# Query, key and value by 26 block products with shared token sums on GpSimd, and every order written anew

## The chip, the core and the metric

The kernel runs on one core of one Trainium2 chip. A core has five engines that run side by side, each through its own queue in the order of the program: TensorE (PE: matrix products into the eight banks of PSUM; its weight loads are shown as PEld), VectorE (DVE), ScalarE (ACT), GpSimd (POOL), and SyncE (SP), whose queue issues nearly all DMA transfers here. The engines wait for one another by semaphores. The metric is the device time of one execution in microseconds.

## The reference

128 graphs of 128 nodes with 512 features go through two layers; all is float32.

```python
# layer 0
h = jnp.maximum(_layernorm(x, axis=-1), 0.0)
q, k, v = (proj(Wq, bq), proj(Wk, bk), proj(Wv, bv))          # 8 heads of 64
scores = jnp.einsum('bhqd,bhkd->bhqk', q, k) * SCALE
scores = scores * (adj + adj)[:, None, :, :]
attn = jax.nn.softmax(scores, axis=-1)
x = x + (jnp.einsum('bhqk,bhkd->bhqd', attn, v) as rows) @ Wo.T + bo
# layer 1
h = jnp.maximum(_layernorm(x, axis=-1), 0.0)
Wh = h @ W;  e = leaky_relu(Wh @ a[:512] + (Wh @ a[512:]).T, 0.2)
attention = softmax(where(adj > 0.5, e, -9e15), axis=1)
x = x + elu(attention @ Wh)
```

(The lines of the softmaxes and of the last sum are shortened here.)

## The kernel before

Graphs are handled in pairs `p` (64 of them) and, for query, key and value, in groups `g` of two pairs (32 of them). A group's normalised and transposed input is the tile `hA`: features on the partitions, four feature blocks of 128, and 256 token columns for each of the two pairs.

The products with `wq`, `wk`, `wv` and, for each pair, with `wo` and `w1` are done by a fast 2x2 scheme. Every matrix is cut into two by two quarters, and seven products of sums of quarters stand for eight plain ones (`PRODUCTS`, L130). The sums of weight quarters are formed once on VectorE (`weight_sum`, L137). The sums of token quarters are formed for each group (`token_sum` called by `hidden_sum`, tile `hS`), and for each pair on the context `cxT` and on the gathered input `gT` (steps `cs`, `gs`). A product of a group is the function `product` (L239 on): four matmuls over 256 columns at L258, accumulated in three banks a, b and c for each of query, key and value. Bank a holds running sums: it is read after four of the seven products, by ScalarE (the function `first`, L270 and L275, with the bias), while banks b and c are added to the result in SBUF by VectorE (`add`, L279), three times for each of query, key and value.

Before these products a pair's input is normalised in its transposed form (`hidden`): step `hd0` subtracts the row means (L222, VectorE, 1024 elements), step `hd1` takes the maximum with zero and multiplies (L224). The rows' statistics come from steps `t0` and `t1` (L165, L166), a small power on GpSimd (L172, L173), and a trip through DRAM (`s0` on GpSimd's queue, `f0` on SP's). Step `sh` adds the vector `c` to a pair's `x` after it was loaded by step `lx` (L234, VectorE).

Attention of a graph (`a` and `b` in step names are the two graphs of a pair): scores (`sc`, L320, two banks), times adjacency (`at`, L327, VectorE), maxima (`mx`, L334), exponentials (`ex`, L339, ScalarE), shares and normalising (`rc` L343, `nm` L348), block transposition on VectorE (`fl`, L355) and through DRAM (`bl`, `pl` on SP's queue), context (`pc`, L388) and its copy by ScalarE into `cxT` (`pe`, L395). Output of layer 0: products `o0` to `o6` (L299), added to `x` by VectorE (`od`, L402). Layer 1: statistics `st`, hidden values `h2` (L418), dot products with the attention vectors (`d`, L425, VectorE), mask, softmax (`wm` L455, `pr` L460, `m1` L464, `e1` L469, `sw` L474 and L475), gathering (`g`, L481, TensorE) and its copy (`ge`, L487), products `w0` to `w6` (L299), collected by ScalarE (`zc`, L495) and VectorE (`wd`, L499), then `ez` (L507), `fa` (L511), `fb` (L515) and the store `so`.

The order of the work on all queues is written out by hand as three lists of steps: `HEAD` once, `ORDER` for each pair `p` from 3 to 59 (the number after the colon is how many pairs behind the step works), and `TAIL` once. Steps `U1` to `U11` are the 21 products of the next group, ten in an even round and eleven in an odd one; `F` and `A` are their takes by ScalarE and VectorE. All PSUM tiles come from one pool of eight banks, `ps1`. TensorE's product waits until the bank it writes is free[...].

Of the kernel before, what the change touches and what calls it, by code (L numbers as in the profile page):

```python
# [8 lines left out]
F32 = mybir.dt.float32  # L9
# [4 lines left out]
P = 128  # L14
# [10 lines left out]
def kernel(  # L25
# [6 lines left out]
    wqT: bass.AP,  # L32
    bq: bass.AP,
    wkT: bass.AP,
    bk: bass.AP,
    wvT: bass.AP,
# [23 lines left out]
    xs, x0s, adjs, adjTs, hAs, hSs = {}, {}, {}, {}, {}, {}  # L60
# [18 lines left out]
    def half_of_hidden(p):  # L79

        g, i = divmod(p, 2)
        if g not in hAs:
            hAs[g] = grp.tile([P, 4, 2, 2 * S], F32, name="hA")
        return hAs[g][:, 2 * i : 2 * i + 2].rearrange("p q c k -> p (q c) k")
# [19 lines left out]
    def column(src, name):  # L104
# [10 lines left out]
    wv_sb, wq_sb, wk_sb, wo_sb, w1_sb = (  # L115
        const.tile([P, 7, 2, E // 2], F32, name=name) for name in ("wv", "wq", "wk", "wo", "w1")
    )
# [16 lines left out]
    FIRSTS = {0: (0, 0), 2: (1, 0), 4: (1, 1), 5: (0, 1)}  # L134
    ADDS = {1: (0, 0, "b"), 4: (1, 1, "c"), 6: (1, 0, "c")}
# [12 lines left out]
    def token_sum(h, s, k):  # L148

        if k == 0:  # L150
            nc.vector.tensor_tensor(s[:, 0], h[:, 2], h[:, 3], OP.add)
        elif k == 1:
            nc.vector.tensor_tensor(s[:, 1], s[:, 0], h[:, 0], OP.subtract)  # L153
        elif k == 2:
            nc.vector.tensor_tensor(s[:, 2], h[:, 0], h[:, 2], OP.subtract)
        else:
            nc.vector.tensor_tensor(h[:, 2], h[:, 1], s[:, 1], OP.subtract)
# [59 lines left out]
    def hidden(p, k):  # L217

        h = hAs[p // 2][:, 2 * (p % 2) : 2 * (p % 2) + 2].rearrange("p q c k -> p (q c) k")
        row = rows0[p][:, None, :, k].to_broadcast([P, 2 * 2, 2 * S])  # L220
        if k == 0:
            nc.vector.tensor_tensor(h, h, row, OP.subtract)  # L222
        else:
            nc.vector.scalar_tensor_tensor(h, h, 0.0, row, op0=OP.max, op1=OP.mult)  # L224

    def hidden_sum(g, k):
        if g not in hSs:
            hSs[g] = grp.tile([P, 3, 2, 2 * S], F32, name="hS")
        token_sum(hAs[g], hSs[g], k)

    def shift(p):


        nc.vector.tensor_tensor(xs[p], xs[p], c_sb[:, None, :].to_broadcast([P, 2, E]), OP.add)  # L234

    accs = {}

    def product(g, which, n):

        if n == 0:  # L240
            if which == "v":
                vs[g] = grp.tile([P, G, E], F32, name="v")
            else:
                qks[g, which] = {}
        if which != "v" and n in (0, 2):
            qks[g, which][n // 2] = grp.tile([P, C, 2 * S], F32, name=which + "T", bufs=3 if which == "q" else 2)
        w = {"q": wq_sb, "k": wk_sb, "v": wv_sb}[which]
        ha, wb, bank = PRODUCTS[n]
        fresh = (g, which, bank) not in accs
        if fresh:  # L250
            accs[g, which, bank] = ps1.tile([P, 2, 2 * S], F32, name="acc_" + bank, tag="ps1")
        acc = accs[g, which, bank]
        h = hAs[g][:, ha] if ha < 4 else hSs[g][:, ha - 4]
        for m in range(2):
            ms = slice(m * P, (m + 1) * P)
            for c in range(2):
                lhsT, rhs = (h[:, c, ms], w[:, wb, c, :]) if which == "v" else (w[:, wb, c, ms], h[:, c, :])
                nc.tensor.matmul(  # L258
                    acc[:, m, :], lhsT, rhs, start=fresh and m == 0 and c == 0, stop=c == 1, skip_group_check=True
                )  # L260

        def dst(t, f):
            if which == "v":
                return vs[g][:, 2 * t : 2 * t + 2, f * 2 * P : (f + 1) * 2 * P]
            return qks[g, which][t][:, 2 * f : 2 * f + 2, :]

        def first(t, f):
            a = accs[g, which, "a"]
            if which == "v":
                nc.scalar.copy(dst(t, f), a)  # L270
            else:
                bias = bk_sb if which == "k" else bq_sb
                for m in range(2):
                    j = 2 * f + m
                    nc.scalar.activation(dst(t, f)[:, m, :], a[:, m, :], AF.Identity, bias=bias[:, j : j + 1])  # L275

        def add(t, f, bank):
            d = dst(t, f)
            nc.vector.tensor_tensor(d, accs[g, which, bank], d, OP.add)  # L279

        def firsts():
            if n in FIRSTS:
                first(*FIRSTS[n])

        def adds():
            if n in ADDS:
                add(*ADDS[n])

        return firsts, adds
# [20 lines left out]
    def scores(b):  # L310
        p, i = divmod(b, 2)
        g, h = divmod(p, 2)
        qT, kT = qks[g, "q"][h], qks[g, "k"][h]
# [80 lines left out]
    def keep_context(b):  # L394
        nc.scalar.copy(rows_of(cxT, b % 2), pcs.pop(b))  # L395
# [88 lines left out]
    def keep_gathered(p, i):  # L484
        if p not in gTs:
            gTs[p] = work.tile([P, 7, 2, S], F32, name="gT")
        nc.scalar.copy(rows_of(gTs[p], i), pgs.pop((p, i)))  # L487
# [77 lines left out]
    SEQ = "v0 v1 v2 v3 v4 q0 v5 q1 v6 q2 q3 q4 k0 q5 k1 q6 k2 k3 k4 k5 k6".split()  # L565
# [6 lines left out]
    EARLY, LATE = 3, 4  # L572

    def listed(text, mark):
# [3 lines left out]
        lx@0 lx@1 Lq1@0 Lq0@0 lx@2 Lk0@0 Lk1@0 Lv0@0 t1@-5 Lo0@0 t0@-5 pp@0 hn0@0 hn1@0 tp0@0 t0@-4 tp1@0 ev0@0 ev1@0  # L578
        t1@-4 U6@-2 Wq0@0 pp@1 Wq1@0 t1@-3 U8@-2 hn0@1 l0@-2 Wq2@0 Lv1@0 hn1@1 tp0@1 Lo1@0 U3@-1 Lw1@0 t0@-3 ev0@1 Lu@0
        Wq3@0 pp@2 tp1@1 hn1@2 U5@-1 ev1@1 hn0@2 F6@-2 Wk0@0 hs0@-3 F3@-1 U1@-2 Wk1@0 hs1@-3 hs2@-3 U10@-2 tp0@2 F10@-2  # L580
        U7@-1 t1@-2 t0@-2 U2@-1 Wv0@0 F7@-1 pp@3 Wk3@0 F1@-2 A8@-2 ev0@2 U9@-1 hn0@3 Wv1@0 hn1@3 hs3@-3 tp0@3 l0@-1
        tp1@2 Wv2@0 la@-1 U3@-2 ev1@2 Lw0@0 ev0@3 lt@0 F9@-1 tp1@3 F2@-1 ccp@0 F3@-2 ev1@3 U1@0 ccd@0 t0@-1 t1@-1 U4@-2
        Wo0@0 l0@0 s0@-1 cu10@0 U5@-2 Wv3@0 A5@-1 U4@-1 hs0@-1 U10@-1 U1@-1 F10@-1 F4@-1 ccs@0 A2@-1 cch@0 sca@0 Wk2@0
        scb@0 ata0@0 ata1@0 U6@-1 mxa@0 hs1@-1 exa2@0 U3@1 t1@0 F5@-2 exa3@0 A6@-1 U6@0 A5@-2 F1@0 Wo1@0 rca1@0 t0@0
        U9@-2 F6@0 l0@1 s0@0 exa1@0 f0@0 exa0@0 U3@0 A9@-2 nma3@0 Wo2@0 nma2@0 rca0@0 cu01@0 U10@0 nma1@0 nma0@0 hs2@-1
        F3@1 U8@0 fla@0 Ww0@0 bla@0 U8@-1 atb0@0 la@0 atb1@0 mxb@0 U5@1 A8@0 exb2@0 A9@-1 pla@0 U2@-2 exb0@0 A5@1 exb1@0
        sh@0 F10@0 U11@-1 exb3@0 rcb1@0 U7@-2 nmb3@0 A11@-1 rcb0@0 t0@1 t1@1 U2@1 F7@-2 nmb1@0 cu11@0 l0@2 s0@1 nmb2@0
        f0@1 U7@1 F3@0 lT@0 cu00@0 nmb0@0 lT@1 sca@1 A2@-2 flb@0 scb@1 pca@0 F7@1 ata0@1 blb@0 ata1@1 F2@1 U5@0 mxa@1
# [91 lines left out]
    def steps(p):  # L680
# [75 lines left out]
        if odd and (g + 2) * 2 < N:  # L756
            for k in range(4):
                table[f"hs{k}"] = lambda k=k: hidden_sum(g + 2, k)
# [70 lines left out]
```

## Time and profile before

| | |
|---|---|
| runs (3) | median 2351.17 us, 2348.68 to 2352.63 |
| profiled execution, span from first to last instruction | 2346.1 us |
| profiled execution, time of its own beside the span | the page gives none |
| TensorE busy | 2332.0 us, 99% |
| VectorE busy | 2000.4 us, 85% |
| ScalarE busy | 1467.2 us, 63% |
| GpSimd busy | 257.0 us, 11% |
| DMA | 314 MB, 134 GB/s over the span |

A line of the timeline gives start and duration in us, engine, line of the kernel, operation, the tile written and the tiles read, shapes, and how many instructions were merged (x8); in brackets stands the idle time before it and what ended it. A float32 matmul appears as two records. The ends of matmuls are modelled, so that a busy TensorE is not TensorE at its peak: the distance from one start to the next tells what a matmul costs.

### The profile page before, as it was taken

To read this page: it belongs to the slowest core of one execution; us is meant where nothing else is said; L and a number is where in the kernel's file an instruction comes from. 1 tells how busy PE (TensorE), PEld (TensorE's weight loads), DVE (VectorE), ACT (ScalarE), POOL (GpSimd) and SP (SyncE) were. 2 spreads that over 40 slices of the span, in tenths; PEclk is the share of its full clock that TensorE was granted. 3 is DMA by queue.
4 is the path that set the end of the run, shared out by engine and by line. 5 is a ranking of instruction groups with operands and counts; after the bars stand their busy time and mean duration, and the time that the engine had idled before them with its cause. 6 is when DMAs were issued, how large, how long until landed. Compare 5 with 4: busy or idle time off the path is not lost.

```text
span 2346.1 us, 41028 instructions
## 1 busy us (share of the span) xinstructions
PE 2332.0 (99%) x14184; PEld 2061.2 (88%) x14184; DVE 2000.4 (85%) x4113; ACT 1467.2 (63%) x4815; POOL 257.0 (11%) x320
## 2 busy tenths in 40 slices
PE   9999999999999999999999999999999999999998
PEld 8888888888888888888888888888888888888886
DVE  6888888888888888888888888888888888888888
ACT  3656666666566665666666666656666566666774
POOL 1101101111101011011110111110101101110000
PEclk9999999999999999999999999999999999999999
DMA  5445454454444554544535445444454453453332
GB/s 171 131 113 157 121 147 120 124 164 125 143 131 119 148 139 130 143 114 142 155 122 149 120 123 165 124 144 131 120 148 137 131 145 108 146 153 116 118 120 95
DMA packets 267351, 314.06 MB, mean 134 GB/s; under 512 B 24200, under 2 KB 192136, under 8 KB 267144
## 3 DMA queue, kind: packets, MB, share of 16 engines
q1 hardware_dynamic: 263112, 311.31, 45.0%
q8 instruction: 112, 1.84, 0.3%
q0 software_dynamic: 1920, 0.13, 0.2%
q14 instruction: 95, 0.78, 0.1%
q10 hardware_dynamic: 2112, 0.01, 0.1%
HBM read 210.51 MB, written 100.85 MB: 133 GB/s over the span
## 4 chain that ended last, share of the span: by engine, by line
PE 99%; DVE 0%; ACT 0%; DMA 0%; issue 0%; POOL 0%; SPq 0%; ACTq 0%; DVEq 0%; POOLq 0%
PE acc_a L258 29%; PE row_a L299 24%; PE acc_c L258 14%; PE row_c L299 9%; PE acc_b L258 7%; PE sc L320 5%; PE pc L388 5%; PE pg L481 5%; PE pt L197 0%; DMA x<-in_x 0%; PE pm L531 0%; DVE st L165 0%; ACT z L495 0%; PE pu L553 0%; DVE z L499 0%
## 5 line engine op out<-in xcount | busy, mean ns | idle before, releaser
L339 ACT ACTIVATE at<-at,nmx 128x128 f32<-128x128 f32 x1024 | 396.3, 390 | 19.8 <-DVE nmx L334 17.9
L348 ACT ACTIVATE at<-at,rs 128x128 f32<-128x128 f32 x1024 | 325.0, 391 | 12.8 <-DVE rs L343 12.1
L299 PE MATMUL row_a<-wo,cxT 128*128 128x256 f32 x1280 | 328.5, 379 | 0.3 <-DVE cxT L153 0.3
L299 PE MATMUL row_a<-w,gT 128*128 128x256 f32 x1280 | 319.4, 380 | 2.9 <-DVE z L499 1.7
L172 POOL TENSOR_SCALAR mv<-mv 128x2 f32<-128x2 f32 x124 | 79.2, 639 | 2016.8 <-DVE mv L166 1994.6
L299 PEld LDWEIGHTS row_a<-w,gT 128*128 128x128 f32 x1280 | 242.3, 190 | 37.9 <-DVE z L499 2.6
L299 PEld LDWEIGHTS row_a<-wo,cxT 128*128 128x128 f32 x1280 | 242.6, 190 | 34.3 <-DVE cxT L153 0.6
L402 DVE TENSOR_TENSOR x<-row_a,x 128x256 f32<-128x256 f32 x320 | 135.3, 423 | 133.1 <-PE row_a L299 129.8
L495 ACT COPY z<-row_a 128x256 f32<-128x256 f32 x256 | 94.3, 368 | 203.7 <-PE row_a L299 203.6
L275 ACT ACTIVATE kT<-acc_a,bk 128x256 f32<-128x256 f32 x256 | 106.5, 466 | 168.2 <-PE acc_a L258 165.0
L327 DVE SCALAR_TENSOR_TENSOR at<-sc,adj 128x512 f32<-128x512 f32 x256 | 165.1, 686 | 42.2 <-PE sc L320 39.8
L339 ACT ACTIVATION_READ_ACCUMULATOR at<-at,nmx 128x1 f32 x1024 | 193.3, 189 | 0.0
L275 ACT ACTIVATE qT<-acc_a,bq 128x256 f32<-128x256 f32 x256 | 106.1, 466 | 123.0 <-PE acc_a L258 123.0
L165 DVE BATCH_NORM_STATS2 st<-x 128x6 f32<-128x512 f32 x256 | 176.1, 688 | 7.4 <-DMA x<-in_x 5.1
L425 DVE SCALAR_TENSOR_TENSOR junk<-h,u 128x512 f32<-128x512 f32 x256 | 173.3, 677 | 0.6
L355 DVE STREAM_TRANSPOSE tr<-at 128x1024 f32<-128x1024 f32 x128 | 158.8, 1240 | 9.2 <-PE pc L388 2.7
L334 DVE TENSOR_REDUCE nmx<-at 128x8 f32<-128x1024 f32 x128 | 156.2, 1220 | 4.3
L487 ACT COPY gT<-pg 128x512 f32<-128x512 f32 x128 | 74.6, 584 | 123.8 <-PE pg L481 117.4
L481 PEld LDWEIGHTS pg<-w,h 128*128 128x128 f32 x1024 | 133.3, 192 | 6.6 <-ACT z L495 0.2
L173 POOL TENSOR_TENSOR mv<-mv,mhalf 128x2 f32<-128x2 f32 x128 | 131.1, 1024 | 30.7 <-DVE mv L168 20.3
L481 PE MATMUL pg<-w,h 128*128 128x128 f32 x1024 | 134.1, 275 | 0.0
L299 PE MATMUL row_c<-w,gT 128*128 128x256 f32 x512 | 133.0, 382 | 0.6 <-DVE z L499 0.5
(130 smaller groups left out, 4876.4 us busy)
## 6 DMA issues: line engine op xcount, KB each, us to landing
blocks<-tr SPq DMA_DIRECT2D x128, 512.0 KB, 6.8
aT<-blocks SPq DMA_DIRECT2D x512, 128.0 KB, 2.9
x<-in_x SPq DMA_DIRECT2D x123, 512.0 KB, 5.0
out<-x SPq DMA_DIRECT2D x63, 512.0 KB, 4.1
hA<-in_xT SPq DMA_DIRECT2D x120, 256.0 KB, 3.7
mr<-rows SPq DMA_DIRECT2D x60, 256.0 KB, 4.4
adj<-in_adj SPq DMA_DIRECT2D x64, 128.0 KB, 4.3
adjT<-in_adjT SPq DMA_DIRECT2D x64, 128.0 KB, 4.2
```

The source lines that it names most:

```text
L165: nc.vector.bn_stats(st, src[:, i, :])
L258: nc.tensor.matmul(acc[:, m, :], lhsT, rhs, start=fresh and m == 0 and c == 0, stop=c == 1, skip_group_check=True)
L275: nc.scalar.activation(dst(t, f)[:, m, :], a[:, m, :], AF.Identity, bias=bias[:, j : j + 1])
L299: nc.tensor.matmul(acc, left[:, la, c, :], w[:, wb, c, :], start=n in (0, 3) and c == 0, stop=c == 1, skip_group_check=True)
L327: nc.vector.scalar_tensor_tensor(ats[b][0][:, k * C : (k + 1) * C, :], scs[b][k], QSCALE, adjs[p][:, i : i + 1, :].to_broadcast([P, C, S]) ...
L334: nc.vector.tensor_reduce(nmx, at, AX.X, OP.max, negate=True)
L339: nc.scalar.activation(at[:, j, :], at[:, j, :], AF.Exp, bias=nmx[:, j : j + 1], accum_out=sums[:, j : j + 1])
L348: nc.scalar.activation(at[:, j, :], at[:, j, :], AF.Copy, scale=rs[:, j : j + 1])
L355: nc.vector.transpose(trs[b], at.rearrange("p h (j k) -> p j h k", k=Q))
L402: nc.vector.tensor_tensor(d, row_acc(p, "o", bank), d, OP.add)
L425: nc.vector.scalar_tensor_tensor(junk, h2[:, i, :], 1.0, u_sb[:, k, :], op0=OP.mult, op1=OP.mult, accum_out=ws[:, i, 1:2] if k else src_sb ...
L481: nc.tensor.matmul(pg[:, c, :], h1s[p][0][:, i, c * P : (c + 1) * P], wts[p][:, i, :], start=True, stop=True)
```

## The change

Query, key and value of a group are computed together by another scheme. The tokens are cut into two halves (the two pairs), the features into four blocks of 128, and the outputs into four blocks of 128. 26 products of one token sum with one weight sum stand for 32 plain ones. `TERMS` lists them in order: the accumulating chain (0 to 3), the number of the token sum, the slot of the weight sum, and where the chain's running value is taken to (token half, output block, sign; a dot takes nothing). `FORMS` lists the 17 token sums; they serve query, key and value alike and are formed by GpSimd, 256 elements each, in eight buffers. `WSUMS` lists the 35 weight sums, formed once by VectorE on the three weights together (384 elements).

Query and key share a bank, value has one of its own. Step `Q` is a product for query and key (two matmuls over 256 columns), step `V` one for value (two matmuls with the token sum as weights over 128 columns). `A` and `B` take the running value: the first time that a part of the result is written ScalarE does it, after that VectorE adds or subtracts.

The row subtraction `hd0` and the addition of `c` (`sh`) go to GpSimd, each in pieces of 512 elements. The token sums of the context and of the gathered input read three of their operands from the PSUM banks rather than from the copy in SBUF. The three lists are new; `ORDER` now covers a whole group, and runs for groups 2 to 28.

```diff
-    wv_sb, wq_sb, wk_sb, wo_sb, w1_sb = (
-        const.tile([P, 7, 2, E // 2], F32, name=name) for name in ("wv", "wq", "wk", "wo", "w1")
-    )
+    wo_sb, w1_sb = (const.tile([P, 7, 2, E // 2], F32, name=name) for name in ("wo", "w1"))
+    w_sb = const.tile([P, SLOTS, 3, P], F32, name="w3")
...
+    TERMS = list(terms("""
+        1,8,7,13- 0,10,18,10- 1,9,19,03- 0,11,0,00- 1,1,20,01+ 0,2,16,. 1,13,5,11+ 0,0,21,03- 1,12,6,12- 0,0,1,02-
+        1,14,14,02- 0,18,24,00+ 0,3,26,01+ 3,20,15,03+ 2,21,22,02- 3,19,25,13+ 2,22,23,12- 3,16,9,11- 2,6,10,.
+        3,17,27,01- 2,4,2,13+ 3,15,4,00- 2,4,3,10- 3,23,12,10- 2,24,8,12+ 2,7,13,11-
+    """))
+    FORMS = list(sums("""
+        4+5 1-8 2+9 0+9 5+7 12-1 3-13 1+2 6+12 16-15 17-3 0-18 16+19 6+19 4-19 7-17 5-1
+    """))
...
+    def load_blocks(n):
+
+        nc.sync.dma_start(w_sb[:, n : C * C : C], wT[:, n : C * C : C])
+
+    def block_sum(k):
+
+        d, a, op, b = WSUMS[k]
+        if op == "n":
+            nc.vector.scalar_tensor_tensor(w_sb[:, d], w_sb[:, a], -1.0, w_sb[:, b], op0=OP.mult, op1=OP.subtract)
+        else:
+            eng = nc.gpsimd if k in () else nc.vector
+            eng.tensor_tensor(w_sb[:, d], w_sb[:, a], w_sb[:, b], OP.add if op == "+" else OP.subtract)
...
-    def token_sum(h, s, k):
+    def token_sum(h, bank, k):
+
+        s = h[:, 4:7]
+
+        def block(q):
+            return bank(q // 2)[:, q % 2 * 2 : q % 2 * 2 + 2, :]
 
         if k == 0:
-            nc.vector.tensor_tensor(s[:, 0], h[:, 2], h[:, 3], OP.add)
+            nc.vector.tensor_tensor(s[:, 0], block(2), h[:, 3], OP.add)
         elif k == 1:
-            nc.vector.tensor_tensor(s[:, 1], s[:, 0], h[:, 0], OP.subtract)
+            nc.vector.tensor_tensor(s[:, 1], s[:, 0], block(0), OP.subtract)
         elif k == 2:
-            nc.vector.tensor_tensor(s[:, 2], h[:, 0], h[:, 2], OP.subtract)
+            nc.vector.tensor_tensor(s[:, 2], block(0), h[:, 2], OP.subtract)
         else:
-            nc.vector.tensor_tensor(h[:, 2], h[:, 1], s[:, 1], OP.subtract)
+            nc.vector.tensor_tensor(h[:, 2], block(1), s[:, 1], OP.subtract)
...
         if k == 0:
-            nc.vector.tensor_tensor(h, h, row, OP.subtract)
+            for c in range(0, C, 2):
+                nc.gpsimd.tensor_tensor(h[:, c : c + 2], h[:, c : c + 2], row[:, c : c + 2], OP.subtract)
...
-        nc.vector.tensor_tensor(xs[p], xs[p], c_sb[:, None, :].to_broadcast([P, 2, E]), OP.add)
+        for i in range(2):
+            nc.gpsimd.tensor_tensor(xs[p][:, i, :], xs[p][:, i, :], c_sb, OP.add)
...
+    def make_form(g, k):
+
+        a, op, b = FORMS[k]
+        forms[g, 2 * C + k] = grp.tile([P, 2 * S], F32, name="tf", bufs=8)
+        eng = nc.gpsimd
+        eng.tensor_tensor(forms[g, 2 * C + k], form(g, a), form(g, b), OP.add if op == "+" else OP.subtract)
...
+    def product_qk(g, n):
+
+        _, f, slot, _ = TERMS[n]
+        acc, fresh = fresh_acc(g, n, "q", [P, 2, 2 * S])
+        for i in range(2):
+            nc.tensor.matmul(
+                acc[:, i, :], w_sb[:, slot, i, :], form(g, f), start=fresh and i == 0, stop=True, skip_group_check=True
+            )
+
+    def product_v(g, n):
+
+        _, f, slot, _ = TERMS[n]
+        acc, fresh = fresh_acc(g, n, "v", [P, 2, P])
+        for i in range(2):
+            nc.tensor.matmul(
+                acc[:, i, :], form(g, f)[:, i * P : (i + 1) * P], w_sb[:, slot, 2, :],
+                start=fresh and i == 0, stop=True, skip_group_check=True,
+            )
+
+    def take_qk(g, n):
+
+        chain, _, _, (t, j, sign) = TERMS[n]
+        acc = accs[g, chain, "q"]
+        if (g, t) not in qks:
+            qks[g, t] = grp.tile([P, 2, C, 2 * S], F32, name="qk", tag=f"qk{t}", bufs=1 + t)
+        d = qks[g, t][:, :, j, :]
+        if (g, t, j) not in begun:
+            begun.add((g, t, j))
+            for i, bias in enumerate((bq_sb, bk_sb)):
+                nc.scalar.activation(d[:, i, :], acc[:, i, :], AF.Identity, bias=bias[:, j : j + 1], scale=float(sign))
+        else:
+            nc.vector.tensor_tensor(d, d, acc, OP.add if sign > 0 else OP.subtract)
+
+    def take_v(g, n):
...
+        if (g, t, j, "v") not in begun:
+            begun.add((g, t, j, "v"))
+            nc.scalar.activation(d, acc, AF.Copy, scale=float(sign))
+        else:
+            nc.vector.tensor_tensor(d, d, acc, OP.add if sign > 0 else OP.subtract)
...
-        nc.scalar.copy(rows_of(cxT, b % 2), pcs.pop(b))
+        nc.scalar.copy(rows_of(cxT, b % 2), pcs[b])
...
-    EARLY, LATE = 3, 4
+    EARLY, LATE = 2, 3
...
     ORDER = """
+        rca1:0 rca0:0 gs1:3 lx:1 sh:1 Q2:0 w0:3 Q25:2 nma2:0 V23:2 B23:2 T7:0 V25:2 A23:2 gs2:3 lt:2 lT:0 f0:0 Q1:0
+        A1:0 B25:2 pca:1 nma3:0 gs3:3 zc0:3 d10:2 d00:2 pcb:1 T5:0 peb:1 nma0:0 pea:1 d11:2 cs0:1 px:2 pd:2 scb:0
...
+        h20:1 d01:1 Q9:0 gs0:2 A9:0 Q10:0 lx:0 T12:0 V13:0 w0:2 Q13:0 zc0:2 B13:0 V15:0 V11:0 B8:0 V10:0 A10:0 t1:-2
+        gs2:2 s0:-1 gs1:2 B11:0 Q11:0 hd0:-1 hd1:-1 w2:2 l0:-3 A11:0 A13:0 h21:1 plb:0 w1:2 V12:0 Q15:0 B10:0 Q12:0
+        wd1:2 s0:-2 f0:-3 exa1:-1 exa0:-1 rca0:-1 exa2:-1 B12:0 exa3:-1 rca1:-1 nma3:-1 d00:1 d10:1 T13:0 Q14:0 A14:0
...
+        exb2:-1 exb3:-1 sh:0 rcb1:-1 cs2:0 exb0:-1 Q19:0 exb1:-1 nmb3:-1 w3:2 T14:0 V16:0 A19:0 od0:0 Q16:0 T0:-2
...
-        for p in range(EARLY, N - LATE):
+        for g in range(EARLY, N // 2 - LATE):
             for step, lag in ORDER:
-                if p >= lag:
-                    do(step, p - lag)
+                do(step, 2 * g - lag)
```

## The prediction

> **What bounds the kernel now.** I read the engines' busy times (part 1) and the chain that ended last (part 4) first, then the windows view over single rounds of the written order, the waits inside one round, and the timeline.
>
> ```profile
> PE 2332.0 (99%) x14184; PEld 2061.2 (88%) x14184; DVE 2000.4 (85%) x4113; ACT 1467.2 (63%) x4815; POOL 257.0 (11%) x320
> PE 99%; DVE 0%; ACT 0%; DMA 0%; issue 0%; POOL 0%; SPq 0%; ACTq 0%; DVEq 0%; POOLq 0%
> ```
>
> The chain is TensorE from end to end. The order repeats every group of four graphs (two pairs); one such round in the windows view (us, then busy us and instructions of PE, PEld, DVE, ACT, POOL):
>
> ```profile
> 1217.39:1289.61 72.22, 72.22 (x442) 64.03 (x441) 62.04 (x128) 45.70 (x151) 8.33 (x11) 1.00 0.47 136
> ```
>
> In that round TensorE waits for nobody; VectorE waits 8.8 us in all, most of it here (waiter, releaser: us, times, longest):
>
> ```profile
> DVE x L402 <- PE row_a L299: 4.3, 4, 2.0
> DVE x L234 <- DMA x<-in_x: 1.9, 1, 1.9
> DVE at L327 <- PE sc L320: 1.3, 2, 0.9
> ```
>
> So VectorE is occupied 72.22 - 8.8 = 63.4 us of 72.2 (88%). Since matmul ends are modelled, I price TensorE by the distance of starts, from its timeline (a float32 matmul is two records):
>
> ```profile
> 1201.84 1.89 PE L258 MATMUL acc_a<-wv,hA 128*128 128x256 f32 x8
> 1203.57 1.89 PE L258 MATMUL acc_b<-hA,wq 128*128 128x256 f32 x8
> ...
> 1216.52 1.05 PE L481 MATMUL pg<-w,h 128*128 128x128 f32 x8
> 1217.41 1.89 PE L258 MATMUL acc_c<-hS,wq 128*128 128x256 f32 x8
> ```
>
> Four matmuls over 256 columns take 1.73 us (0.432 each), four over 128 columns, each with new weights, 0.89 us (0.222 each). VectorE's start distances, back to back, are likewise shorter than its durations:
>
> ```profile
> 1203.67 0.42 DVE L499 TENSOR_TENSOR z<-row_c,z 128x256 f32<-128x256 f32 x1
> 1204.00 0.68 DVE L279 TENSOR_TENSOR v<-acc_c,v 128x512 f32<-128x512 f32 x1
> 1204.60 0.68 DVE L279 TENSOR_TENSOR v<-acc_b,v 128x512 f32<-128x512 f32 x1
> ```
>
> 256 elements cost 0.33 us, 512 cost 0.60, and 1024 (L334 at 1222.64, next start 1223.78) 1.14.
>
> [...]
>
> ```profile
> 1217.14 1.19 DVE L511 SCALAR_TENSOR_TENSOR x<-z,x 128x1024 f32<-128x1024 f32 x1
> 1217.39 1.02 POOL L172 TENSOR_SCALAR mv<-mv 128x2 f32<-128x2 f32 x1 [22.98 <-DVE mv L166]
> 1228.52 0.30 POOL L172 TENSOR_SCALAR mv<-mv 128x2 f32<-128x2 f32 x1 [8.27 <-DVE mv L166]
> ```
>
> The two-number operation takes 0.30 us alone and 1.02 under L511, ending just after it. That VectorE is held up by GpSimd no row shows: today's GpSimd work is too short. [...]
>
> **The change, part by part, per round.**
>
> TensorE. Out: 21 products of four 256-column matmuls, 21 x 1.73 = 36.3 us. In: 26 products, each two matmuls of 256 (query, key) and two of 128 columns (value): 26 x (0.865 + 0.445) = 34.1. All else stays. A round bound by TensorE becomes 72.2 - 2.2 = 70.0; over 32 groups 70 us.
>
> VectorE. Out: nine additions of 512 (L279, 5.4 us), four token sums of 512 (L151 to L157, 2.4), two row subtractions of 1024 (L222, 2.3), two additions of c (L234, 2.3): 12.4. In: 24 of the 26 products are taken; eight go to ScalarE, 16 to VectorE, once with 512 and once with 256 elements: 16 x 0.93 = 14.9. Occupied 63.4 + 2.5 = 65.9 us, 94% of 70.0. The context's and gathered sums keep their price (L499, with PSUM input, is as long as L151).
>
> ScalarE. Query and key firsts stay at 16 of 256; value goes from four of 512 to eight of 256: under 1 us more on 46 of 70. Nothing.
>
> GpSimd. In: 17 forms of 256, four row subtractions and four c additions of 512. [...] It is not the bound.
>
> [...] VectorE keeps 18 instructions with two SBUF inputs a round: eight L425, two L224, four L511/L515, two L455, two L475. Below: nothing, as no row shows it. [...] the list puts few forms beside such instructions (T5 and T13 beside d00, d10, d11; the rest stand beside takes). [...]
>
> New waits. hd1 on VectorE follows hd0, now on GpSimd; behind it in VectorE's queue stand A11 and A13, and Q12 and Q15 on TensorE wait for these, with only w2, w1 and V12 (2.2 us) between Q11 and Q15. sh on GpSimd waits for the load of x (1.9 us a round at L234 today); behind it T7 or T14, which TensorE needs later. Each product waits until its bank's last sum is taken. A gathered or context bank, free today after ScalarE's copy, is now held until gs3 or cs3. Counting in the written order each bank from first matmul to last reader, weighted with TensorE's time, the mean goes from 5.8 to 6.6 of eight banks; with seven or eight in use it is 26% now and 59% after. A late VectorE step therefore reaches TensorE sooner. TensorE's own loss is about 0.3 us a round today: 21 x 1.73, 28 row products x 0.865, four L481 groups x 0.89, four score groups x 1.0 and four context groups x 0.95 make 71.9 of 72.2; I take 0.8 more, worked from nothing but these two loads, with 0 and 4 as ends.
>
> Head. 35 block sums of 384 elements (0.47 us) replace 12 of 512: 16.5 for 7.2 us, before and among the first products, and the first needs blocks from three loads where the first needed one weight. Adding the rows for all steps of the head's list, VectorE has 102 us beside TensorE's 121 now, and 159 beside 152 after; with the start at 5 to 10 us that leaves TensorE some 8 us later (0 to 20). The tail has the same proportions (132 to 140, then 192 to 205): nothing. DMA volume is the same.
>
> Sum: 32 x (2.2 - 0.8) = 45, less 8, is 37 us off the profiled span of 2346.1: 2309. The page gives no time of its own beside the span; the runs' median 2351.2 is 5 above it. Predicted 2314.
>
> **Rivals.**
> A. Full gain: no loss to VectorE, head 2: 2346 - 70 + 2 + 5 = 2283. For: rounds repeat to 0.01 us, so an order that fits once fits always. Against: 94% and fuller banks.
> B. VectorE becomes the bound (ends slower). [...] It decides where VectorE's work plus its waits pass 72.0 a round. Against: much of the waiting is being early, which a fuller engine isn't.
> C. Forms late: GpSimd in order behind sh and hd0[...].
> D. The narrow matmuls do no good, since a weight load lasts 190 ns and a 128-column pass streams in 111: 104 loads x 0.08 = +8 us a round, about 2570. L481's start distance speaks against it.
>
> **How the numbers follow.** Likeliest (TensorE still the bound with some loss, 2290 to 2335) 0.55; A 0.13; B 0.24; C 0.06; D 0.02. A measurement of this kernel can tell about 0.2%, 5 us. Faster: 0.55 + 0.13 + 0.02 of B's mild end = 0.70; same 0.05 (B and C near 72.2 a round); slower 0.25. The range leaves out A's lowest third, B's upper half and D: 2283 to 2390; the likeliest case's own is 2290 to 2335.
>
> **What would show it.** Right: rounds of 70.3 to 71.5 us, TensorE's chain still over 95%, four value matmuls at 0.89 us, VectorE occupied 66 to 68 a round[...]. Wrong: TensorE's waits for VectorE adding to over 2 us a round, L425 or L511 longer than 0.68 and 1.2 us, VectorE in the chain, TensorE waiting for "tf", a first product after 20 us.

## The result, and the profile after

The kernel after takes 2441.74 us (median of four runs, 2439.01 to 2443.41) against 2351.67 us before: ratio 1.0381, 95% interval 1.0367 to 1.0396. It is 90 us slower, where 37 us less were predicted.

The page of the kernel after, parts 1 (busy times), 4 (the chain that ended last) and 5 (the group of the dot products, now L472: busy us, mean ns of one, idle time before):

```profile
PE 2324.4 (95%) x15464; PEld 2050.1 (84%) x15464; DVE 2250.1 (92%) x4620; ACT 1471.9 (60%) x4943; POOL 914.3 (37%) x1112
...
PE 75%; DVE 18%; ACT 3%; issue 2%; DMA 1%; DVEq 0%; SPq 0%; ACTq 0%
...
L472 DVE SCALAR_TENSOR_TENSOR junk<-h,u 128x512 f32<-128x512 f32 x256 | 334.2, 1305 | 14.0 <-ACT h L465 8.4
```

TensorE's chain has holes now, and VectorE fills them. The dot products, same line and same size as L425 before, take twice their 677 ns. One round of the written order, in the windows view (the last three numbers are the granted TensorE clock, the DMA share and GB/s):

```profile
1205.10:1279.85 74.75, 71.73 (x482) 63.54 (x481) 69.51 (x143) 45.70 (x154) 28.77 (x36) 1.00 0.45 132
```

A round takes 74.75 us, 2.5 more than before; 27 rounds make 71 us of the 94 by which the span grew. Before the rounds settle the start loses 16 (12.8 up to the first mask, L502, and 2.8 in the round after it), and the tail 8. TensorE's waits over the whole span (waiter, releaser: us, times, longest):

```profile
PE acc_q L297 <- DVE gT L191: 49.6, 27, 1.8
PE sc L367 <- DVE gT L197: 13.3, 24, 1.2
PE pc L435 <- DMA aT<-blocks: 12.2, 21, 0.9
...
PE acc_q L297 <- DVE qk L323: 7.3, 1, 7.3
```

The waits name short VectorE instructions (L191 lasts 0.41 us). What makes them late stands ahead of them in VectorE's queue. In the timeline of one round the eight dots take 2.95, 1.09, 0.68, 1.02, 1.02, 0.69, 0.69 and 2.90 us, 11.0 together for 5.4 undisturbed. The two long ones, with what GpSimd did at the time:

```profile
1207.25 2.95 DVE L472 SCALAR_TENSOR_TENSOR junk<-h,u 128x512 f32<-128x512 f32 x1
...
1204.30 0.77 POOL L248 DMA_DIRECT2D rows<-mv  x1 [0.29 <-POOL mv L213]
1205.10 0.74 POOL L282 TENSOR_TENSOR tf<-hA,tf 128x256 f32<-128x256 f32 x1
1205.79 2.49 POOL L270 TENSOR_TENSOR x<-x,c 128x512 f32<-128x512 f32 x2
1208.24 0.72 POOL L282 TENSOR_TENSOR tf<-hA,tf 128x256 f32<-128x256 f32 x1
1208.93 0.72 POOL L282 TENSOR_TENSOR tf<-hA 128x256 f32<-128x256 f32 x1
1209.72 2.20 POOL L282 TENSOR_TENSOR tf<-hA,tf 128x256 f32<-128x256 f32 x2
...
1272.65 2.90 DVE L472 SCALAR_TENSOR_TENSOR junk<-h,u 128x512 f32<-128x512 f32 x1 [0.30 <-ACT h L465]
...
1271.66 0.77 POOL L248 DMA_DIRECT2D rows<-mv  x1 [0.30 <-POOL mv L213]
1272.46 2.54 POOL L263 TENSOR_TENSOR hA<-hA,mr 128x512 f32<-128x512 f32 x2
```

Each long dot ends half a microsecond or so after GpSimd's row of operations does, at 1275.00 in the second case, and in the first at a gap of 0.07 us at 1209.65. GpSimd is far ahead of its place in the list: `sh:0` is written some 40 steps behind `d00:1`, and runs before it. The start shows the same thing at its plainest:

```profile
101.67 8.07 DVE L179 TENSOR_TENSOR wo<-wo 128x512 f32<-128x512 f32 x1
...
101.03 0.77 POOL L248 DMA_DIRECT2D rows<-mv  x1 [0.29 <-POOL mv L213]
101.83 7.35 POOL L270 TENSOR_TENSOR x<-x,c 128x512 f32<-128x512 f32 x6
...
110.39 2.08 PE L297 MATMUL acc_q<-hA,w 128*128 128x256 f32 x4 [7.28 <-DVE qk L323]
```

One weight sum of 512 elements lasts 8.07 us instead of 0.67, under six additions in a row, and TensorE waits 7.28 us for the take behind it.

### The profile page after: what moved, and what is told of

The parts are those of the page before. It is cut to its first block, busy times and chain, and to the rows that moved or that the text cites. A ratio compares the mean times of both kernels' runs of the same rounds, so it can differ in the third digit from the quotient of the medians.

```text
span 2440.5 us, 45674 instructions
## 1 busy us (share of the span) xinstructions
PE 2324.4 (95%) x15464; PEld 2050.1 (84%) x15464; DVE 2250.1 (92%) x4620; ACT 1471.9 (60%) x4943; POOL 914.3 (37%) x1112
## 3 DMA queue, kind: packets, MB, share of 16 engines
q8 instruction: 123, 2.02, 0.4%
## 4 chain that ended last, share of the span: by engine, by line
PE 75%; DVE 18%; ACT 3%; issue 2%; DMA 1%; DVEq 0%; SPq 0%; ACTq 0%
PE acc_q L297 22%; PE row_a L346 19%; PE acc_v L306 12%; PE row_c L346 9%; DVE junk L472 8%; PE sc L367 6%; PE pg L528 5%; DVE qk L323 3%; PE pc L435 3%; DVE v L336 2%; DVE hA L265 1%; ACT h L465 1%; ACT v L334 1%; DVE st L205 1%; ACT gT L534 1%
## 5 line engine op out<-in xcount | busy, mean ns | idle before, releaser
L297 PE MATMUL acc_q<-tf,w 128*128 128x256 f32 x2176 | 559.8, 383 | 50.7 <-DVE gT L191 49.6
L297 PEld LDWEIGHTS acc_q<-tf,w 128*128 128x128 f32 x2176 | 388.4, 191 | 104.9 <-ACT h L465 59.7
L282 POOL TENSOR_TENSOR tf<-hA,tf 128x256 f32<-128x256 f32 x288 | 229.9, 802 | 443.3 <-PE acc_v L306 259.6
L323 DVE TENSOR_TENSOR qk<-qk,acc_q 128x512 f32<-128x512 f32 x512 | 342.1, 674 | 28.1 <-PE acc_q L297 27.6
L472 DVE SCALAR_TENSOR_TENSOR junk<-h,u 128x512 f32<-128x512 f32 x256 | 334.2, 1305 | 14.0 <-ACT h L465 8.4
L306 PEld LDWEIGHTS acc_v<-w,tf 128*128 128x128 f32 x2176 | 311.3, 191 | 25.8 <-DVE v L336 0.8
L306 PE MATMUL acc_v<-w,tf 128*128 128x128 f32 x2176 | 322.7, 276 | 0.2 <-DVE v L336 0.2
L297 PE MATMUL acc_q<-hA,w 128*128 128x256 f32 x1152 | 300.8, 384 | 7.3 <-DVE qk L323 7.3
L336 DVE TENSOR_TENSOR v<-v,acc_v 128x256 f32<-128x256 f32 x512 | 209.8, 411 | 34.7 <-PE acc_v L306 34.6
L297 PEld LDWEIGHTS acc_q<-hA,w 128*128 128x128 f32 x1152 | 207.4, 191 | 34.7 <-DVE qk L323 8.6
L270 POOL TENSOR_TENSOR x<-x,c 128x512 f32<-128x512 f32 x128 | 160.7, 1279 | 61.1 <-DMA x<-in_x 43.3
```

The source lines that it names most:

```text
L270: nc.gpsimd.tensor_tensor(xs[p][:, i, :], xs[p][:, i, :], c_sb, OP.add)
L282: eng.tensor_tensor(forms[g, 2 * C + k], form(g, a), form(g, b), OP.add if op == "+" else OP.subtract)
L297: nc.tensor.matmul(acc[:, i, :], w_sb[:, slot, i, :], form(g, f), start=fresh and i == 0, stop=True, skip_group_check=True)
L306: nc.tensor.matmul(acc[:, i, :], form(g, f)[:, i * P : (i + 1) * P], w_sb[:, slot, 2, :], start=fresh and i == 0, stop=True, skip_group_ch ...
L323: nc.vector.tensor_tensor(d, d, acc, OP.add if sign > 0 else OP.subtract)
L336: nc.vector.tensor_tensor(d, d, acc, OP.add if sign > 0 else OP.subtract)
```

## The experiments

The first theory was that a VectorE instruction with two operands in SBUF waits for a whole run of back-to-back GpSimd operations. Rival 1: VectorE simply has too much work. Rival 2: the token sums read from PSUM hold banks that TensorE needs.

**The dots with one operand in SBUF.**

```diff
-        nc.vector.scalar_tensor_tensor(junk, h2[:, i, :], 1.0, u_sb[:, k, :], ..., accum_out=...)
+        nc.vector.bn_stats(ws[:, i, 0:6] if k else src_sb[:, i, 0:6], h2[:, i, :])
```

> The eight dot products a round on VectorE (L472, two operands in SBUF, 5.4 us if nothing delays them, 11.0 us in the profile after) become eight statistics of the same 512 elements with one operand in SBUF (0.6 us each by L205). The dot products' values are left out. Theory 1, VectorE instructions with two SBUF operands wait for whole runs of GpSimd operations: none of the eight is longer than 0.75 us, a round 70.2 to 71.0 us in place of 74.75, the time 2310 to 2340. Rival 1, VectorE simply has too much work: its work is the same, so 2430 to 2445. Rival 2, the sums read from PSUM hold banks that TensorE needs: banks and sums are the same, so 2430 to 2445.

Measured: 2367.8 us, 74 below the kernel after (ratio to before 1.0084, 1.0061 to 1.0107), but above the 2310 to 2340 expected. The better rounds take 70.8 to 71.2 us, but others reach 75.4. With one operand in SBUF these 74 us go, for as many instructions of the same 512 elements, so the long waits are not the work's; the unevenness is something else: TensorE's context product waits 17.0 us in all for the turned blocks (`aT`), up to 2.9 at a time.

**The dots later in the list.**

```diff
-  exa3:-1 rca1:-1 nma3:-1 d00:1 d10:1 T13:0 Q14:0 A14:0 px:1 gs3:2 A12:0 pca:0 pcb:0 pd:1
+  exa3:-1 rca1:-1 nma3:-1 T13:0 Q14:0 A14:0 gs3:2 A12:0 pca:0 pcb:0
...
-  B15:0 peb:0 ... lt:1 d11:1
+  B15:0 d00:1 d10:1 px:1 pd:1 peb:0 ... lt:1 d11:1 d01:1
```

> Only the written order of the repeating round changes: two dot products (d00, d10 of the pair before) and the two steps that follow them stand about 5 us later, after GpSimd's run of forms and c additions, and one (d01) stands beside d11. Work, engines and banks are the same. Theory 1: the dots of 2.95 and 2.90 us become 0.7, a round 70.3 to 71.2 us, the time 2315 to 2345, which is below the kernel before. Rival 1 and rival 2: the amount of work and the banks' sums are the same, 2430 to 2450.

Measured: 2391.57 us (1.0169, 1.0154 to 1.0185), 50 below the kernel after with nothing but places changed. The dots' mean falls from 1305 to 799 ns; rounds are 72.1 to 75.3 us. The direction was right, the size half: four dots within 6 us now make TensorE wait 0.4 to 1.1 us a round for a take behind them (`acc_q` for `qk`, 20.6 us in all, 7.3 of them in the start as before).

**Row subtractions and additions of c back on VectorE.**

```diff
-                nc.gpsimd.tensor_tensor(h[:, c : c + 2], h[:, c : c + 2], row[:, c : c + 2], OP.subtract)
+                nc.vector.tensor_tensor(h[:, c : c + 2], h[:, c : c + 2], row[:, c : c + 2], OP.subtract)
...
-            nc.gpsimd.tensor_tensor(xs[p][:, i, :], xs[p][:, i, :], c_sb, OP.add)
+            nc.vector.tensor_tensor(xs[p][:, i, :], xs[p][:, i, :], c_sb, OP.add)
```

> The row subtractions and the additions of c go back from GpSimd to VectorE, eight instructions of 512 elements a round, 4.9 us; the forms stay on GpSimd. Theory 1: the runs of GpSimd lose their long members, the dots shrink from 11.0 to 6.5 us or less a round, VectorE is busy 69 to 70 us of a round of 70.5 to 72.5; the time 2325 to 2380, below the kernel after in spite of more work on VectorE. Rival 1: VectorE has 74 us of work a round and more than that in waits, 2520 to 2600. Rival 2: the bank waits stay, 2440 to 2560. A third rival, hd0 and sh come late from GpSimd and hd1 or the forms wait for them: 2330 to 2400 too, but with the dots as long as after.

Measured: 2454.84 us (1.0441, 1.0425 to 1.0456): a miss. The dots do shrink to 717 ns, but one of the two `hd1` of each round (L265) now takes 2.5 us instead of 1.2. It meets the same thing as the long dots: an issue of GpSimd, L248, with two forms right behind it. TensorE then waits some 1.9 us a round for the take behind this `hd1` (last line, over the whole span):

```profile
1204.95 2.48 DVE L265 SCALAR_TENSOR_TENSOR hA<-hA,mr 128x1024 f32<-128x1024 f32 x1
...
1204.12 0.77 POOL L248 DMA_DIRECT2D rows<-mv  x1 [0.29 <-POOL mv L213]
1204.92 1.41 POOL L282 TENSOR_TENSOR tf<-hA,tf 128x256 f32<-128x256 f32 x2
...
PE acc_q L297 <- DVE qk L323: 52.7, 27, 2.0
```

The expectation had also added wrongly: 65.9 us of the prediction and 4.9 are 70.8, more than TensorE's 70. The windows view of a round of this kernel:

```profile
1200.00:1274.23 74.23, 71.50 (x481) 63.42 (x480) 71.12 (x151) 45.62 (x155) 18.26 (x28) 1.00 0.45 132
```

With 71.12 us of VectorE in it a round takes 74.2 to 76.2, but 1.3 of the 71.12 are the delay of that one `hd1`. So this run does not show that the amount of work by itself, rival 1, bounds a round: work and delay come together here.

**Token sums from the copies in SBUF.**

```diff
-            return bank(q // 2)[:, q % 2 * 2 : q % 2 * 2 + 2, :]
+            return h[:, q]
```

> The token sums of the context and of the gathered rows read ScalarE's copies in SBUF again and no longer the PSUM banks (one copy of the first groups moved ahead of a sum that needs it). Rival 2: the banks come free earlier, TensorE's waits for the sums go, a round 71 to 72 us, 2340 to 2370. Theory 1: eight more instructions of 256 elements a round with two SBUF operands, which can meet GpSimd's runs; 0 to 3 us a round longer, 2435 to 2530. Rival 1: 2435 to 2450.

Measured: 2492.15 us (1.0604, 1.0589 to 1.062), rounds of 76.65. Rival 2 falls: reading the banks is worth 50 us. All four instructions of each sum read a bank, so it is 16 instructions a round that now read SBUF alone, not the eight of the expectation. They take 83 us longer in all (`L197` on the context takes 807 ns from SBUF on average, 411 from PSUM).

**The blocks' transfers earlier.** On top of the dots later, `plb:0` stands right behind `lx:0`. Before, its transfers queued on SP behind `l0:-3`, which waits for VectorE's statistics.

> As the kernel with the dots later, and the four transfers of the turned attention blocks (plb) stand right behind lx in the written order, no longer behind a load (l0) that waits on SP's queue for VectorE's statistics. Theory: the irregular part of the rounds with the dots later (72.1 to 75.3 us) is TensorE's context product waiting for these transfers; with them earlier nearly all rounds are 72.0 to 72.6 us, and the time is 2365 to 2378 in place of 2391.6. Rival: the transfers are late for another reason, such as their own time, 2385 to 2395.

Measured: 2381.87 us (1.0133, 1.0118 to 1.0148). Nearly every round is 72.59 us now: the unevenness was this wait. The total fell short of the expectation by 4 us.

**More places changed.**

```diff
-  d10:2 d00:2 pcb:1 T5:0 peb:1 nma0:0 pea:1 d11:2 cs0:1 px:2 pd:2 scb:0 pv:2 A25:2
+  pcb:1 T5:0 peb:1 nma0:0 pea:1 cs0:1 scb:0 A25:2 d10:2 d00:2 px:2 pd:2 d11:2 pv:2
...
-  o3:0 Q18:0 pv:1 wm:1
+  o3:0 Q18:0 pv:1 d01:1 wm:1
```

> As the one before, and further: d01 stands ahead of wm and no longer in a row with three other dots; d10, d00, d11 of the other pair stand some 2 us later, after GpSimd's run of c additions and forms; one weight sum of the start (Wo2, 8.07 us in the profile after) stands where GpSimd is idle. Theory 1[...]: rounds 70.6 to 71.6 us, the start 8 to 10 us shorter, 2325 to 2350, below the kernel before. Rival 1, VectorE's amount of work: at 94% it keeps TensorE at 72 us a round wherever the instructions stand, 2360 to 2375.

Measured: 2370.43 us (1.0084, 1.0067 to 1.0101). Rounds stay at 72.6; only the start is shorter. A miss for theory 1, and rival 1's number. TensorE still waits 1.1 us a round for the take behind `d00:1` and `d10:1`; the best order below, with these two back in their place and the issue elsewhere, takes 71.4 us, so the same amount of work doesn't by itself force 72.6.

**One word of the start moved.**

```diff
-  hd0@1 hd1@1 T0@2 ... peb@0 Wo2@0 exb1@1
+  hd0@1 Wo2@0 hd1@1 T0@2 ... peb@0 exb1@1
```

> As the kernel after, with a single word of the start's list moved: the weight sum Wo2 (one VectorE instruction of 512 elements, 8.07 us in the profile after under six GpSimd additions in a row) stands some 10 us earlier, where GpSimd is idle. Theory 1: it lasts 0.7 us, TensorE's wait of 7.3 us goes, 2431 to 2436. Rival, the start is bound by VectorE's work anyway and the time gained is lost at the next wait: 2439 to 2443.

Measured: 2432.04 us (1.0348, 1.0333 to 1.0364), 9.7 below the kernel after, as expected. The wait of 7.28 us costs more than itself: behind it two matmuls over 256 columns, 0.87 us elsewhere, take 2.0 (110.39 to 112.39).

**The runs by themselves.** A kernel of small trials: GpSimd adds a column to n rows of 512 elements, and a VectorE addition of 512 starts inside.

```diff
+        for i in range(n):
+            nc.gpsimd.tensor_tensor(rows[i][:, :size], rows[i][:, :size], go.to_broadcast([P, size]), OP.add)
...
+                nc.vector.tensor_tensor(d, other, src_a, OP.add)
```

> The whole computation is left out. Ten small trials, three times each: GpSimd runs n operations of 512 elements back to back (1.25 us each), and a VectorE instruction of 512 elements starts inside the run. Theory 1: with two SBUF operands it lasts as long as the rest of the run, about 1 us for n=1, 2 for n=2, 4.5 for n=4, 9 for n=8; with one operand in PSUM, or with one SBUF operand only, 0.7 us. Rival, taking turns instruction by instruction: never over 2 us whatever n is. [...] Eight GpSimd operations of 256: as n=4 by theory 1. Four against four: one side ends wholly first by theory 1, both last some 6 us if they take turns. One GpSimd operation started inside eight VectorE instructions: about 5 us if the keeping is mutual, under 2 us[...].

Measured: whatever n is, VectorE's instruction takes 0.83 us at most (0.98 beside eight operations of 256). For n=8, in the timeline:

```profile
16.51 8.46 POOL L63 TENSOR_TENSOR row<-row,go 128x512 f32<-128x512 f32 x8 [0.41 <-ACT go L85]
...
17.26 0.83 DVE L74 TENSOR_TENSOR two<-other,srca 128x512 f32<-128x512 f32 x1
```

Theory 1 as it stood is wrong: the two take turns, instruction by instruction. Four against four last 5.17 and 5.37 us.

**With two whole rows on GpSimd.** Theory 1a: with two whole rows as GpSimd's operands VectorE is held over the whole run. (The new line is shortened.)

```diff
-            nc.gpsimd.tensor_tensor(rows[i][:, :size], rows[i][:, :size], go.to_broadcast([P, size]), OP.add)
+            nc.gpsimd.tensor_tensor(rows[i][:, :size], rows[i][:, :size], full[:, :size], OP.add)
```

> The whole computation is left out. In the trials before, where GpSimd's second operand was one column spread over the row (1.04 us an operation), VectorE's instruction with two SBUF operands lasted 0.83 us at most, whatever the length of the run: theory 1 is wrong for that form. Here GpSimd adds two whole rows of 512 elements, as the c additions and the forms of the kernel do; one trial (spread4) keeps the column. Theory 1a[...]: 2 us for n=2, 4.5 for n=4, 9 for n=8, spread4 0.83. Rival, they take turns here too and the long waits of the kernel have another cause: never over 2 us. Trials with one operand in PSUM or one operand only: 0.7 by both.

Measured: 1.32 us for n=2, 4 and 8, so turns again. With one operand in PSUM 0.67, with one operand only 0.68. Theory 1a falls too. That left the question what the three long waits of the kernel had in common. Sorting all delayed instructions of a round by what GpSimd had done just before gave it: each long one meets a row of operations that begins right behind L248, a transfer that GpSimd issues itself. The others, delayed by 0.3 to 0.6 us, do not.

**An issue ahead of the run.** Theory 1b: behind a transfer that GpSimd issues, VectorE is held until GpSimd has nothing queued.

```diff
+            nc.gpsimd.dma_start(dram.tile([P, 1], F32, name="col"), go)
         for i in range(n):
             nc.gpsimd.tensor_tensor(rows[i][:, :size], rows[i][:, :size], full[:, :size], OP.add)
```

> The whole computation is left out. Without a transfer, runs of GpSimd gave VectorE a turn after one operation (1.33 us at most). In the kernel after, each VectorE instruction that was held over a whole run (2.95, 2.90 and 8.07 us) met a run that begins right behind a transfer that GpSimd issues itself (rows, L248); those behind other work were held for one operation. Theory 1b[...]. Then, with an issue of a one-column transfer ahead of the run: none4 (no issue) 1.3 us, two1 1.3, two2 2.5, two4 5, two8 10, half8 6, gap4 5 to 6, bank4 and one4 0.7, both4 the four of VectorE end after the four of GpSimd, and pause4, where GpSimd waits for ScalarE between issue and run, 1.3. Rival: the issue doesn't matter and all of them stay at 1.4 or less.

Measured, in each of three repetitions: 2.4 us for n=2, 4.8 for n=4, 9.65 for n=8, 5.4 for eight operations of 256 and 5.2 with one-element operations between; without the issue, at n=4, 1.7 at most. The timeline for n=8, for n=4 with an operand in PSUM, and for n=4 with GpSimd waiting for ScalarE between issue and run:

```profile
35.99 0.56 POOL L68 DMA_DIRECT2D col<-go  x1 [2.26 <-ACT go L98]
36.57 9.79 POOL L75 TENSOR_TENSOR row<-row,full 128x512 f32<-128x512 f32 x8
37.26 9.65 DVE L86 TENSOR_TENSOR two<-other,srca 128x512 f32<-128x512 f32 x1
...
48.25 4.92 POOL L75 TENSOR_TENSOR row<-row,full 128x512 f32<-128x512 f32 x4
48.94 0.67 DVE L88 TENSOR_TENSOR bank<-bank,srca 128x512 f32<-128x512 f32 x1
...
89.82 5.37 POOL L75 TENSOR_TENSOR row<-row,full 128x512 f32<-128x512 f32 x4
90.94 0.69 DVE L86 TENSOR_TENSOR pause<-other,srca 128x512 f32<-128x512 f32 x1
```

At n=4 the issue decides between 1.69 and 4.79 us in the same kernel, at n=8 between the 1.32 of the trial before and 9.65. Four VectorE instructions against four of GpSimd end after them, 6.96 us. So the trials bear out theory 1b for the operations queued right behind an issue: at n=8 VectorE's addition (37.26 to 46.91) ends 0.55 us after the whole run (46.36). Only the trial with the wait differs, 0.69 us where 1.3 was expected.

**The issue on ScalarE's queue, at the same place.**

```diff
-            nc.gpsimd.dma_start(rows0[p].rearrange("b p s -> p b s"), mv)
+            nc.scalar.dma_start(rows0[p].rearrange("b p s -> p b s"), mv)
```

> As the kernel after, with one word changed: the transfer of a pair's row statistics (rows, L248, two numbers a row) is issued on ScalarE's queue instead of GpSimd's. GpSimd's operations, VectorE's work and the written order are the same. Theory 1b: every dot takes 1.1 us or less, the weight sum of 8.07 us likewise, most rounds 70.8 to 72 us, the time 2355 to 2385. Theory 1 without the issue's part[...] and rivals 1 and 2: 2435 to 2445.

Measured: 2411.91 us (1.026, 1.0245 to 1.0276), 30 below the kernel after but 27 above the expected interval. The dots above 2 us, 54 in the kernel after, are gone, and the weight sum of 8.07 us takes 0.85. But the longest dot takes 1.78 us, not the 1.1 expected: it starts just behind the start of a GpSimd operation of 512 elements and waits for nearly all of it. Rounds are 72.5 to 76.8, with 34.4 us of waiting for the turned blocks.

> As the one before, and the four transfers of the turned attention blocks (plb) stand right behind lx in the written order. Theory 1b, with the late transfers as what showed next: regular rounds of 70.6 to 71.3 us and a time of 2330 to 2355. Rival 1, VectorE's amount of work bounds a round near 72.6 us as in the kernel with the steps spread: 2365 to 2385.

Measured, with `plb` earlier on top: 2361.03 us (1.0041, 1.0027 to 1.0055), regular rounds of 72.02; 6 us above the expectation. In both, ScalarE now stands in front of the issue until GpSimd has taken the power. Its waits in the second of the two (waiter, releaser: us, times, longest):

```profile
ACT at L386 <- POOL mv L213: 66.2, 27, 2.5
```

**The issue alone, later in the round.** The issue becomes a step of its own; nothing else moves but the fetch `f0` behind it.

```diff
-  wd1:2 s0:-2 f0:-3 exa1:-1 exa0:-1 rca0:-1 exa2:-1 B12:0 exa3:-1 rca1:-1 nma3:-1
+  wd1:2 s0:-2 exa1:-1 exa0:-1 rca0:-1 exa2:-1 B12:0 exa3:-1 rca1:-1 sd:-1 nma3:-1
...
-  pea:0 A15:0
+  pea:0 sd:-2 f0:-3 A15:0
```

> As the kernel after, with the row statistics' transfer issued on ScalarE's queue as a step of its own (sd) that stands later in the repeating round than the power on GpSimd; nothing else is moved. Theory 1b: dots of 1.1 us at most, no 8.07 us sum, no wait of ScalarE for GpSimd; rounds of 71.0 to 73 us, uneven where the turned blocks come late; 2360 to 2390. Without the issue's part: 2435 to 2445.

Measured: 2373.04 us (1.0091, 1.0074 to 1.0108), inside the interval. Undoing this one thing takes back 69 of the 90 us, with VectorE's work, engines and order as in the kernel after. Queue and place of the issue changed together here; at the old place, in the run with ScalarE's queue above, where ScalarE waits in front of it, it was 30. No dot is above 2 us any more, but as there the longest is 1.78, and the mean still 1.02 us: the 1.1 us expected as the most was a miss.

**The best order.** Issue late on ScalarE, `plb` earlier, `d01` ahead of `wm`, the other pair's dots 2 us later, `Wo2` moved; `d00:1` and `d10:1` stand where the change put them.

> As the kernel with the issue on ScalarE and the blocks earlier, and in the written order: the issue is a step of its own (sd) and stands later than the statistics' power, so that ScalarE doesn't wait for GpSimd in front of it; d01 stands ahead of wm; d10, d00, d11 of the other pair stand 2 us later; the weight sum Wo2 stands where GpSimd is idle. If the remaining 2 us a round are order: rounds of 70.4 to 71.3 us, 2320 to 2345, below the kernel before. If they are VectorE's amount of work (rival 1): rounds of 71.8 to 72.6, 2350 to 2370.

Measured: 2346.06 us (ratio to before 0.9977, 0.9969 to 0.9985): below both kernels, by 0.2% from the one before, and 1 us above the interval expected. Rounds take 71.42 us. Busy times, chain, and one round of the windows view:

```profile
PE 2315.0 (99%) x15464; PEld 2048.2 (87%) x15464; DVE 2117.4 (90%) x4620; ACT 1462.3 (62%) x4943; POOL 881.0 (38%) x1052
...
PE 87%; DVE 9%; ACT 1%; issue 1%; POOL 1%; DMA 0%; DVEq 0%; SPq 0%; ACTq 0%; POOLq 0%
```

```profile
1943.00:2014.42 71.42, 71.36 (x482) 63.42 (x481) 65.07 (x143) 45.38 (x156) 27.95 (x34) 1.00 0.50 137
```

VectorE's busy time in a round is 4.4 us less than in the kernel after, for the same 143 instructions. What is gained in 27 rounds (0.8 us each, 22 in all) is mostly paid in the start (13 us up to the settled rounds) and the tail (7).

**The start in another order.** The first pair's normalised rows and transposes ahead of the statistics that wait for a load.

> As the one before, with the first steps of the start in another order: the first pair's normalised rows and their transposes ahead of the statistics that wait for the third pair's load, and the first block sums ahead of the fourth pair's statistics. If TensorE's first wait (6.1 us for hn) is order: 4 to 10 us less than the one before. If the loads of the weight blocks bound the start: within 2 us of it.

Measured: 2348.93 us (0.9993, 0.9984 to 1.0002), 3 more than without, which is neither of the two cases. TensorE waits 6.7 us ahead of its first product, now with no releaser shown. The order of these steps isn't what bounds the start; whether it is the loads of the weight blocks was not tested by itself.

**The issue moved in the kernel before.** The same word as above, in the kernel before.

> The kernel before with one word changed, the issue of the row statistics' transfer on ScalarE's queue instead of GpSimd's. Theory 1b: before the change GpSimd has nothing of length behind the issue, so no VectorE instruction is held; 2346 to 2356, no difference. Rival: the kernel before paid for the issue too, 2320 to 2343.

Measured: 2381.2 us (1.0126, 1.011 to 1.0141), 30 more: a miss. Here too ScalarE waits for GpSimd in front of the issue:

```profile
ACT z L495 <- POOL mv L173: 97.7, 56, 1.8
```

On the question that it was run for it answers all the same: the dots (L425) take 677 ns on average with the issue on either engine, so the kernel before was not held up by it.

**The best order with the issue back on GpSimd.**

> The best order so far with one word changed back: its later step sd issues on GpSimd's queue again. Theory 1b: the two issues now stand ahead of T13 and ahead of the c additions; if VectorE's two dots meet the run behind them they take 2 to 3 us again, rounds of 73 to 74.5 us, 2390 to 2430; if they fall beside it, 2343 to 2360, and then the profile must show no VectorE instruction with two SBUF operands inside such a run.

Measured: 2358.93 us (1.0032, 1.002 to 1.0044), 13 more than with ScalarE, rounds of 72.17. The time lies in the second interval, but its condition fails: one dot a round does meet a run, in its middle, and is held for what is left of the two additions (2.02 us; in the best order with ScalarE's issue the dots take 0.74 on average). The added step shifts the line numbers: L251 is the issue, L273 the addition of c, L475 the dot:

```profile
1232.67 0.72 POOL L251 DMA_DIRECT2D rows<-mv  x1
1233.42 2.51 POOL L273 TENSOR_TENSOR x<-x,c 128x512 f32<-128x512 f32 x2
...
1234.49 2.02 DVE L475 SCALAR_TENSOR_TENSOR junk<-h,u 128x512 f32<-128x512 f32 x1
```

## Why the prediction was wrong

**TensorE: right.** 26 products were priced so that a round bound by TensorE takes 70.0 us. At the prediction's own prices the products of a round add up to 69.6 us, and with the 0.3 that the round before lost to 69.9. A value product of two narrow matmuls takes 0.44 us (101.64 to 102.08), as priced, so rival D falls.

**VectorE: right in amount.** 65.9 us occupied were expected; the best order's round of 71.42 less 5.3 of VectorE's waits is 66.1. GpSimd is not the bound, as the prediction says, though no row before the change shows an operation of such length: forms take 0.73 us and operations of 512 take 1.25, 28.8 us in the round of 74.75. TensorE waits 0.54 us at most for a form (in the start of the best order): rival C did not come.

**GpSimd holding VectorE: the step that failed.** No row before the change shows it, as the prediction says, and what the prediction allowed for it was the author's estimate, with no measured number behind it. Measured in a round of the kernel after are 5.6 us in the dots and 0.55 in L459, 6.2 together. (The 18 instructions also left out the two L412, now L459, on two numbers a row.) Two things are wrong in the step. The first is the length of a hold. While the engines take turns it is small: 0.3 to 0.6 us in the kernel after, 1.1 at most where the issue is on ScalarE's queue, and in the trials without an issue a VectorE addition of 0.67 us took 1.32 in runs of one to eight operations, and 1.69 at most; with an operand in PSUM it took 0.67 there too, and statistics with a single operand 0.68. Behind an issue from GpSimd's own queue a hold lasts over the run: 9.65 us over eight operations. Two dots, 2.22 to 2.27 us late, make 4.5 of the 6.2.

The second is the reading of the list: "the list puts few forms beside such instructions". The list gives the order on each engine, not the time. GpSimd runs ahead until a buffer or a load stops it (in the kernel after it waits 903.8 us in all for TensorE to be done with a form's buffer, and 43.3 for loads of `x`), and so `sh:0` and four forms, written behind the dots, ran under them. The step `s0`, whose issue is L248, stood on GpSimd's queue before as well and was not costed.

**New waits.** "hd1 follows hd0" and the fuller banks were priced at 0.8 us in all. The kernel after loses 4.8 a round against 70.0. The best order, without the holds, loses 1.4, nearly twice the estimate and inside its ends of 0 and 4; so most of the loss was no new wait, but the delay of the held dots passed on through banks held longer: `acc_q` waits for L191 with 1.8 us right behind the dot of 2.90.

**Start and tail.** The first product at 20.1 us instead of 11.4 is the 8 us foreseen. The weight sum of 8.07 us was not; it is the same failed step in the start, and moving that one word took 9.7 us off. The tail loses 8 us where nothing was expected, and 32 groups were multiplied where 27 run at a full round's length. So the sum was off apart from the holds too: even the best order's span, 2344.7, is 36 us above the 2309 predicted. The rounds make 23 of them (45 us less were expected in 32 rounds, 22 came in 27), the tail 7 and the start 5.

**The rivals.** B is nearest: VectorE enters the chain, and a round is 74.75 us. Its point of decision, work plus waits over 72.0, is passed. But its cause, the sum of work, is not shown by itself in any run; in the kernel with the rows back on VectorE an issue of GpSimd holds VectorE too. A was not reached: even the best order is at 71.42, not 70.0. Of the signs of being wrong all but one came: TensorE's waits for VectorE (2.3 us in the round shown), the dot of 1305 ns, VectorE in the chain, the first product at 20.1 us; in the kernel after TensorE did not wait for a form.

**What stays open.** What ends a hold. In the small trials it was the run's end, or a step that waits for ScalarE; in the kernel once a gap of 0.07 us, once, with the issue back on GpSimd, the end of two operations with a form right behind. What share of the 69 us is the queue of the issue and what its later place was not tested by itself. Why the best order still loses 1.4 us a round, and the start 13 us, was not followed further.

## What to carry to other kernels

Work moved to GpSimd can run far ahead of its place in a written order (here some 40 steps), so look at what it does at the time, not in the list, and keep VectorE instructions with two SBUF operands away from it, or give them an operand in PSUM (0.67 us instead of 4.79 behind an issue with four additions). Do not let GpSimd issue a transfer right ahead of such work (4.79 us with the issue, 1.69 at most without); issue it from another queue, and late enough that this engine doesn't wait in front of it (ScalarE waited 66.2 us in all where it did). When many waits name short instructions (49.6 us named one of 0.41), look one or two places up in the releaser's queue for the one that is too long (a dot of 2.90).

## What was not expected of the hardware

- After a transfer of one column issued by GpSimd, a VectorE addition of 512 elements took 9.65 us beside eight GpSimd additions; without the issue 1.32. What in the issue causes it is not shown.
- Two streamed rows cost a GpSimd addition 1.22 us, a row and a column 1.03.
- After TensorE's wait of 7.28 us the next two matmuls over 256 columns took 2.0 us instead of 0.87, at a granted clock of 0.50 (1.00 in the round shown).
